# A state-space scan with two attention and feed-forward layers: the last feed-forward chunk on two row tiles, and the attention sums one step later

## The chip, the core and the metric

The kernel runs on one core of a Trainium2 chip. A core has five engines with queues of their own: PE, the matrix engine (its weight loads are listed as PEld); DVE, the vector engine; ACT, the scalar engine; POOL, the general engine (GpSimd); and SP (SyncE), which here only issues transfers. Each takes its instructions in the order in which they were queued, and they meet at semaphores. Operands lie in on-chip memory (SBUF); PE writes into accumulator banks (PSUM). The metric is the device time of one execution, in microseconds (us).

## The reference

The input `x` holds 32 sequences of 256 tokens with 256 features, in fp32. The result is `x` plus what two stages make of it. Cut to what matters:

```python
# stage 1, once: a gated state-space block
xr, gate = split(x @ W_in.T); xr = xr + cond[:, None, :]
xn = layernorm(silu(causal_conv4(xr)))               # 512 channels
Bm, Cm, dt = split(xn @ W_xproj.T)                   # 16 states each
h = clip(h * (1 + dt*A) + Bd * xn_t, -10, 10)        # 256 steps, one after another
y = (C_t . h + D * xn) * silu(gate) @ W_out.T

# stage 2, two layers of:
q, k, v = split(shift_token(y) @ wqkv)               # 8 heads of 64
q, k = rotary_xpos(l2norm(q) * qs, l2norm(k) * ks)
y = y + softmax(local_mask(8 * q @ k.T)) @ v @ wo     # windows of 128, each sees the one before
h = layernorm(shift_token(y)) * lg + lb
a, g = split(h @ w1 + b1)                            # 682 each
y = y + (a * gelu(g)) @ w2 + b2                      # 682 -> 256
```

## The kernel before

**Groups and the order of work.** The 32 sequences are handled in four groups of eight (`GB`). A generator, `group_scan`, emits stage 1 of one group as an agenda of small pieces, in chunks of 32 time steps. Another, `blocks`, emits stage 2 of a group and yields after each slot of work. `side_by_side` runs the two together: while `blocks` does the layers of group g, pieces of the scan of group g+1 are emitted between its slots, about one and a half per slot. So the scan of group 0 runs alone at the start, three groups have a scan beside them, and the last group has none. The order in which a queue gets its instructions follows from this emission; the tile framework, which adds the semaphores, moves some of them a little.

**Attention.** `blocks` goes over the eight sequences `b` of the group (L1184). Work for b and b+1 is mixed in eight slots, so that PE has other work while the remaining engines prepare what it needs next:

- slots 1, 2, 4, 5 project v, q and k of sequence b+1, window by window (`project_qkv`, L736). `rotated` (L745 to L770) then makes the normalised and rotated q or k: a square on ACT (L749), multiplies and sums on DVE (L752, L757, L762, L766), an addition, a power and a multiply on POOL (L760, L768, L769).
- `turn(b, w)` transposes the rotated q and k of one window on PE (L775), and ACT copies them out of PSUM (L780). Window 1 of b is turned in slot 1 of b; window 0 of b+1 in slot 8 of b.
- slot 3 divides sequence b-1 by its sums (`divide`, PE L994, DVE L1002), and computes scores; `scores` (L926 to L952) first puts the mask into the bank with a bf16 matmul (L934), then runs heads in pairs, one on rows 0 to 63 and one on rows 64 to 127 of the array (L941). ACT takes the exponential (L950). The last scores come in slot 6.
- slot 6 also runs `finish(b-1)`, the output projection (L786) and its addition to the residual.
- slot 7 runs `sums(b)`: PE adds the exponentials over the keys (`rs`, L960) and DVE takes the reciprocal (L968); and `values(b)`: the exponentials times v (`ov`, L979), copied by ACT (L986).

For the last two sequences of a group the first two sequences of the feed-forward are prepared in the same slots. `normalise(0, n)` transposes the residual (`tp_h`, L1019), takes mean and variance on DVE, the inverse root on POOL (L1029), and normalises (`hn`, DVE L1031). `spread(0, n)` transposes the result back (`tp_hn`, L1044).

**Feed-forward.** `feed_forward` takes two sequences at a time (index j, 512 tokens). The 682 hidden columns are cut into `MCH`, five chunks of 128 and one of 42 rows (`MREM`). `widen(j, m)` computes both halves of chunk m (L1066), ACT applies gelu (L1074), and DVE multiplies, giving `ag` (L1076). `narrow(j, m)` multiplies `ag` with `w2` into two PSUM banks `po_f0` and `po_f1`, one for each half of the 256 output features (L1087), added up over the six chunks. It runs one chunk behind `widen`, except that the last chunk follows at once: `widen(j, 5)`, then `narrow(j, 4)`, then `narrow(j, 5)`. In the last pair of a layer the first projections of the next layer and a `turn` come in between (`lead_in`). In `widen` the 42-row chunk already keeps both halves side by side, on two column tiles: one at rows 0 to 41 of a bank, the other from row `DH` = 64.

**Weights.** `ff_weights` (L1146) loads `w1` and `w2` of a layer, one buffer each, by SP (L1137). Behind them in SP's queue are the loads `xrep` (L538), which bring the scan its next rows.

An fp32 matmul is executed as two passes, each with its own weight load, so counts of PE instructions in the profile are twice those in the code.

Of the kernel before, what the change touches and what calls it, by code (L numbers as in the profile page):

```python
# [14 lines left out]
ALU = mybir.AluOpType  # L15
# [4 lines left out]
P = 128  # L20
S = 256
DM = 256
KM = DM // P
# [14 lines left out]
DH = 64  # L38
W = 128
NW = S // W  # L40
HID = 682
MCH = [(o, min(P, HID - o)) for o in range(0, HID, P)]
MREM = MCH[-1][1]
# [30 lines left out]
def kernel(  # L74
# [29 lines left out]
    nc = tc.nc  # L104
# [5 lines left out]
    def loaded(src, shape, name, q=None):  # L110
        t = const.tile(shape, FP, tag=name, name=name)
        (q or nc.scalar).dma_start(out=t, in_=src)
        return t
# [18 lines left out]
    b1_sb = loaded(b1, [P, L, 2, len(MCH)], "b1_sb")  # L132
# [20 lines left out]
    for j in range(NJ):  # L153
# [25 lines left out]
        out=mask_t[:, 0:W], in_=mask_t[:, 0:W], compare_op=ALU.is_ge, fill=MASKED_LOW,  # L179
# [3 lines left out]
        out=mask_t[:, W : 2 * W], in_=mask_t[:, W : 2 * W], compare_op=ALU.is_ge,  # L183
# [9 lines left out]
    for h in range(HEADS):  # L193
# [7 lines left out]
        out=b1g_sb[DH : DH + MREM], in_=b1[0:MREM, :, 1, len(MCH) - 1]  # L201
# [12 lines left out]
    with tc.tile_pool(name="setup", bufs=2) as setup, tc.tile_pool(  # L214
# [3 lines left out]
        for src, pos, dst in ((qk_scale, rot_c, rc_sb), (qk_scale_sw, rot_s, rs_sb)):  # L218
            tab = setup.tile([P, NW, 2, DH], FP, tag="tab", name="tab")
            nc.scalar.dma_start(out=tab, in_=pos)  # L220
            for l in range(L):
                sc = setup.tile([P, 2 * DH], FP, tag="qk_sc", name="qk_sc")
                nc.scalar.dma_start(
                    out=sc, in_=src[l].rearrange("a d -> (a d)").partition_broadcast(P)
# [63 lines left out]
    def program(ctx, exact):  # L288
# [12 lines left out]
        def bank(pool, tag, name):  # L301
            return pool.tile([P, DI], FP, tag=tag, name=name)
# [493 lines left out]
        if exact:  # L796
# [4 lines left out]
                out=mask[:, 0:W], in_=mask[:, 0:W], compare_op=ALU.is_ge, fill=MASKED,  # L801
# [3 lines left out]
                out=mask[:, W : 2 * W], in_=mask[:, W : 2 * W], compare_op=ALU.is_ge, fill=MASKED,  # L805
# [201 lines left out]
        class FeedForward:  # L1007
# [46 lines left out]
            def widen(self, j, m):  # L1054
                l, (o, n) = self.l, MCH[m]
                pa = bank(ps_w, "w", "pa")
                if n == P:
                    pg, b1g = bank(ps_w, "w", "pg"), b1_sb[0:n, l, 1, m : m + 1]
                    order = [(x, k) for x in (1, 0) for k in range(KM)]
                else:  # L1060

                    pg, b1g = pa[DH : DH + n], b1g_sb[DH : DH + n, l : l + 1]
                    order = [(x, k) for k in range(KM) for x in (1, 0)]
                for half_, k in order:
                    ps = pg if half_ else pa
                    nc.tensor.matmul(  # L1066
                        ps[0:n, :],
                        self.w1[:, k, half_ * HID + o : half_ * HID + o + n],
                        self.h[j][:, k].rearrange("p b t -> p (b t)"),
                        start=(k == 0),  # L1070
                        stop=(k == KM - 1),
                    )
                gl = aw.tile([P, 2 * S], FP, tag="pT", name="gl", bufs=6)
                nc.scalar.activation(gl[0:n, :], pg[0:n, :], AF.Gelu, bias=b1g)  # L1074
                ag = aw.tile([P, 2 * S], FP, tag="pT", name="ag", bufs=6)
                nc.vector.scalar_tensor_tensor(  # L1076
                    ag[0:n, :], pa[0:n, :], b1_sb[0:n, l, 0, m : m + 1], gl[0:n, :],
                    ALU.add, ALU.mult,
                )
                self.ag[m] = ag  # L1080

            def narrow(self, j, m):
                if m == 0:
                    self.po = [bank(ps_w, "w", f"po_f{d}") for d in range(KM)]
                n = MCH[m][1]
                for d in range(KM):
                    nc.tensor.matmul(  # L1087
                        self.po[d],
                        self.w2[0:n, m, d * P : (d + 1) * P],
                        self.ag[m][0:n, :],  # L1090
                        start=(m == 0),
                        stop=(m == len(MCH) - 1),
                    )
                if m < len(MCH) - 1:
                    return
                l, b0 = self.l, self.g * GB + 2 * j
                for d in range(KM):
                    po = self.po[d].rearrange("p (b t) -> p b t", b=2)
                    rv = self.res[j][:, d, :, 1:]
                    if l < L - 1:  # L1100
                        nc.vector.scalar_tensor_tensor(
                            rv, po, b2_sb[:, l, d : d + 1], rv, ALU.add, ALU.add
                        )
                    else:
                        xs = ap_.tile([P, 2, S], FP, tag="rot", name="xs", bufs=4)
                        nc.sync.dma_start(out=xs, in_=xT[:, d, b0 : b0 + 2, :])
                        fo = ap_.tile([P, 2, S], FP, tag="swp", name="fo", bufs=3)
                        nc.vector.scalar_tensor_tensor(
                            fo, po, b2_sb[:, l, d : d + 1], rv, ALU.add, ALU.add
                        )  # L1110
                        nc.gpsimd.tensor_add(fo, fo, xs)
                        nc.sync.dma_start(out=outT[:, d, b0 : b0 + 2, :], in_=fo)
# [22 lines left out]
        def weights(src, l, shape, name):  # L1135
            t = wpool.tile(shape, FP, tag=name, name=name)
            nc.sync.dma_start(out=t, in_=src[:, l])  # L1137
            return t

        def attention_weights(l):  # L1140
            return (
                weights(wqkv, l, [P, KM, 3 * DI], "wqkv_sb"),
                weights(wo, l, [P, NC_, DM], "wo_sb"),
            )

        def ff_weights(l):  # L1146
            return (
                weights(w1, l, [P, KM, 2 * HID], "w1_sb"),
                weights(w2, l, [P, len(MCH), DM], "w2_sb"),
            )  # L1150

        def scratch(g):
            return dp.tile([P, KM, GB, S], FP, tag="ys", name="ys", bufs=2)
# [26 lines left out]
        def blocks(g, at, nxt):  # L1180

            for l in range(L):
                ff = FeedForward(g, l, at.res, *ff_weights(l))
                for b in range(GB):  # L1184
                    more = b + 1 < GB
                    more and at.project(b + 1, 0, 2)
                    at.turn(b, 1)
                    yield
                    more and at.project(b + 1, 0, 0)
                    more and at.project(b + 1, 0, 1)  # L1190
                    yield
                    b > 0 and at.divide(b - 1)
                    at.scores(b, 1, 0, HEADS // 2)
                    yield
                    at.scores(b, 0, 0, 2)
                    more and at.project(b + 1, 1, 2)
                    yield
                    more and at.project(b + 1, 1, 0)
                    more and at.project(b + 1, 1, 1)
                    yield  # L1200
                    at.scores(b, 0, 2, 2)
                    b > 0 and at.finish(b - 1)
                    if b >= GB - 2:
                        ff.normalise(0, 2 * (b - GB + 2))
                    yield
                    at.sums(b)
                    at.values(b)
                    if b >= GB - 2:
                        ff.normalise(0, 2 * (b - GB + 2) + 1)
                        ff.spread(0, 2 * (b - GB + 2))  # L1210
                    yield
                    more and at.turn(b + 1, 0)
                    if b >= GB - 2:
                        ff.spread(0, 2 * (b - GB + 2) + 1)
                    yield
                yield
                at.divide(GB - 1)
                yield
                res, follow = at.res, None

                def last(m):
                    nonlocal follow
                    if m == 0:
                        if l + 1 < L:
                            follow = Attention(l + 1, res, *attention_weights(l + 1))
                        else:
                            follow = nxt()
                    if follow is not None:
                        lead_in(follow, m)

                pieces = feed_forward(ff, last)
                next(pieces)
                at.finish(GB - 1)
                yield
                for _ in pieces:
                    yield
                at = follow
            state_at[0] = at
# [3 lines left out]
        for _ in group_scan(0, ys):  # L1242
            pass
        at = Attention(
            0, [load_res(ys, j) for j in range(GB // 2)], *attention_weights(0)
        )
        for m in range(6):
            lead_in(at, m)
        for g in range(NG):
            if g + 1 < NG:  # L1250
# [3 lines left out]
                def nxt():  # L1254
                    return Attention(
                        0, [load_res(ys, j) for j in range(GB // 2)], *attention_weights(0)
                    )
# [4 lines left out]
            at = state_at[0]  # L1262
# [119 lines left out]
```

## Time and profile before

Three runs took 4258.27, 4266.41 and 4266.48 us; the median is 4266.41. The profiled execution took 4264.77 us, with a span of 4262.5.

| engine | busy us | share of the span |
|---|---|---|
| PE | 3885.2 | 91% |
| DVE | 2600.1 | 61% |
| ACT | 1744.2 | 41% |
| POOL | 1684.0 | 40% |

| stretch, us | what runs | PE busy, us |
|---|---|---|
| 0 to 510 | the scan of group 0 alone | 379.1 |
| 510 to 3565 | groups 0 to 2, each beside the scan of the next | 2829.0 |
| 3565 to 4262 | group 3 alone | 677.1 |

How to read the lines that follow. A line of the list of groups has the source line, the engine, the operation, what it writes and reads, shapes and count; then busy time and the mean length of one in ns; then the idle time of the engine ahead of it and what ended it. A line of the waits has who waited, for whom, total us, how often, and the longest. A line of the timeline has start, length, engine, line, operation and count. Passes on PE overlap in the pipeline: the length of one is more than the distance to the next start, and the distance is what a pass costs. `42*128` is rows times columns of the array that are used.

### The profile page before, as it was taken

The numbers are of one execution on the slowest core, as the hardware profiler recorded it, in microseconds if no ns is written. First come the engines' busy times: TensorE is split into PE (matmuls) and PEld (weight loads), VectorE is DVE, ScalarE is ACT, GpSimd is POOL, SyncE is SP. The second block draws the span as 40 slices with busy tenths as digits, with TensorE's granted clock in tenths as the row PEclk, the third lists the DMA queues.
The fourth block names the chain that finished last, engine by engine and source line by source line (L and its number), as shares of the span: only waits on it lengthen the run. The fifth ranks groups of instructions, "written<-read, shape, count | busy, mean of one in ns | idle before, by whom it ended". The sixth has DMA issues, their size and how long they took to land. (4 is left out here: it accounts for less than half of the span.)

```text
span 4262.5 us, 51606 instructions
## 1 busy us (share of the span) xinstructions
PE 3885.2 (91%) x17980; PEld 2003.9 (47%) x17980; DVE 2600.1 (61%) x4952; ACT 1744.2 (41%) x3217; POOL 1684.0 (40%) x1749
## 2 busy tenths in 40 slices
PE   5777799898898999999899999999989899999999
PEld 2222255544455445544455445554455544654653
DVE  5777557666676546766776645766677653443442
ACT  2554335443444334443444423544344433322331
POOL 3333165323553156422555126532355314523531
PEclk9899999999999999999999999999999999999999
DMA  5777603443334312443433521344333431000000
GB/s 150 178 185 180 155 24 85 119 104 105 92 92 120 100 57 56 111 108 94 115 95 96 140 67 39 85 119 104 105 95 90 127 95 51 1 20 21 1 10 31
DMA packets 266114, 386.30 MB, mean 91 GB/s; under 512 B 161779, under 2 KB 170996, under 8 KB 263668
## 3 DMA queue, kind: packets, MB, share of 16 engines
q1 hardware_dynamic: 261776, 380.86, 34.1%
q8 instruction: 145, 2.38, 0.2%
q10 hardware_dynamic: 4068, 2.04, 0.2%
q14 instruction: 125, 1.02, 0.1%
HBM read 347.70 MB, written 33.55 MB: 89 GB/s over the span
## 5 line engine op out<-in xcount | busy, mean ns | idle before, releaser
L543 ACT ACTIVATE xrep<-xrep,beta 128x512 f32<-128x512 f32 x1024 | 693.1, 715 | 929.2 <-DMA xrep<-xnd 797.2
L550 DVE CUSTOM_DVE_ANT_0 h<-h,xrep,lim 128x512 f32<-128x512 f32 x1024 | 916.4, 895 | 149.7 <-ACT xrep L543 58.5
L736 PE MATMUL ps_qkv<-wqkv_sb,res 128*128 128x512 f32 x1536 | 733.6, 616 | 16.9 <-DMA res<-ys 6.3
L760 POOL TENSOR_TENSOR rot<-rot,swp 128x512 f32<-128x512 f32 x256 | 331.1, 1293 | 586.8 <-DVE swp L757 503.5
L736 PEld LDWEIGHTS ps_qkv<-wqkv_sb,res 128*128 128x128 f32 x1536 | 287.5, 196 | 359.4 <-issue 303.3
L562 PE MATMUL y<-h,ly 128*32 128x512 f32 x2048 | 411.3, 632 | 48.9 <-DVE h L550 48.0
L768 POOL TENSOR_TENSOR rn<-ss,neg_half 128x8 f32<-128x8 f32 x256 | 434.2, 1696 | 26.5 <-DVE ss L766 14.1
L1087 PE MATMUL po_f<-ag,w_sb 128*128 128x512 f32 (+1 forms) x768 | 378.8, 617 | 37.8 <-DVE ag L1076 37.8
L752 DVE TENSOR_TENSOR rot<-ps_qkv,rc_sb 128x512 f32<-128x512 f32 x256 | 175.6, 686 | 369.2 <-ACT sq L749 369.0
L326 PE MATMUL ps_in<-xg,w_in_sb 128*128 128x256 f32 x1024 | 393.0, 517 | 1.8 <-DMA xg<-in_xT_dram 1.5
L1066 PE MATMUL pa<-hT,w_sb 128*128 128x512 f32 (+1 forms) x896 | 363.8, 596 | 0.0
L1076 DVE SCALAR_TENSOR_TENSOR ag<-pa,b_sb,gl 128x512 f32<-128x512 f32 x192 | 143.4, 747 | 329.9 <-PE pa L1066 210.3
L1066 PE MATMUL pg<-hT,w_sb 128*128 128x512 f32 x640 | 313.7, 613 | 0.0
L769 POOL TENSOR_TENSOR rot<-rot,rn 128x512 f32<-128x512 f32 x256 | 276.7, 1081 | 19.1
L326 PEld LDWEIGHTS ps_in<-xg,w_in_sb 128*128 128x128 f32 x1024 | 190.1, 199 | 187.4 <-issue 127.1
L1029 POOL TENSOR_TENSOR rstd<-ve,neg_half 128x1 f32<-128x1 f32 x128 | 76.5, 598 | 508.1 <-DVE ve L1027 494.5
L373 DVE SCALAR_TENSOR_TENSOR acc<-xr,wc_sb,acc 128x256 f32<-128x256 f32 x384 | 190.0, 506 | 126.7 <-POOL acc L362 122.7
L1087 PEld LDWEIGHTS po_f<-ag,w_sb 128*128 128x128 f32 (+1 forms) x768 | 141.6, 194 | 229.4 <-issue 143.6
L950 ACT ACTIVATE pT<-sc 128x512 f32<-128x512 f32 x384 | 206.2, 590 | 97.1 <-PE sc L941 96.4
L786 PE MATMUL ps_wo<-oT,wo_sb 128*128 128x256 f32 x1024 | 237.3, 385 | 0.0
L583 POOL TENSOR_TENSOR xd<-xd,dskip_sb 128x512 f32<-128x512 f32 x64 | 86.8, 1357 | 367.1 <-DMA xd<-xnd 202.4
L749 ACT ACTIVATE sq<-ps_qkv 128x512 f32<-128x512 f32 x256 | 148.9, 594 | 200.7 <-PE ps_qkv L736 147.5
(144 smaller groups left out, 5444.2 us busy)
## 6 DMA issues: line engine op xcount, KB each, us to landing
xrep<-xnd SPq DMA_DIRECT2D x512, 512.0 KB
xnd<-xn SPq DMA_DIRECT2D x64, 256.0 KB
xd<-xnd SPq DMA_DIRECT2D x256, 64.0 KB
wqkv_sb<-in_wqkv_dram SPq DMA_DIRECT2D x8, 1536.0 KB
w_sb<-in_w_dram SPq DMA_DIRECT2D x8, 1364.0 KB
xg<-in_xT_dram SPq DMA_DIRECT2D x64, 128.0 KB
ys<-yo SPq DMA_DIRECT2D x64, 128.0 KB
res<-ys SPq DMA_DIRECT2D x32, 256.0 KB
```

Source lines behind the costliest of these rows:

```text
L326: nc.tensor.matmul(ps, w_in_sb[:, k, ch * P : (ch + 1) * P], x, start=(k == 0), stop=(k == KM - 1),)
L543: nc.scalar.activation(bx, bx, AF.Copy, scale=ck[c]["beta"][:, t : t + 1])
L550: nc.vector._custom_dve(TENSOR_ADD_SAT, out=h_new, in0=state["h"], in1=bx, s0=ck[c]["lim"][:, 0, t : t + 1], s1=ck[c]["lim"][:, 1, t : t + 1],
L562: nc.tensor.matmul(ck[c]["y", hb][32 * q : 32 * q + 32, :], ly[hb % 2][:, 32 * t : 32 * t + 32], ck[c].pop(("h", hb * TB + t)), start=(i = ...
L736: nc.tensor.matmul(ps, res[b // 2][:, k, b % 2, t0 : t0 + W], wqkv_sb[:, k, a * DI : (a + 1) * DI], start=(k == 0), stop=(k == KM - 1),)
L760: nc.gpsimd.tensor_add(rot, rot, swp)
L768: nc.gpsimd.tensor_tensor(rn, ss, neg_half, ALU.pow)
L769: nc.gpsimd.tensor_mul(rot, rot, bc(rn, 2, DH))
L786: nc.tensor.matmul(po[:, d], wo_sb[:, c, d * P : (d + 1) * P], oT[:, c, :], start=(c == 0), stop=(c == NC_ - 1),)
L950: nc.scalar.activation(p, banks[r], AF.Exp)
L1066: nc.tensor.matmul(ps[0:n, :], self.w1[:, k, half_ * HID + o : half_ * HID + o + n], self.h[j][:, k].rearrange("p b t -> p (b t)"), start= ...
L1087: nc.tensor.matmul(self.po[d], self.w2[0:n, m, d * P : (d + 1) * P], self.ag[m][0:n, :], start=(m == 0), stop=(m == len(MCH) - 1),)
```

## The change

It has two parts, and a transfer that the first needs.

The first part puts the second matmul of the 42-row chunk on two row tiles of the array. Until now both outputs read rows 0 to 41. Now output 0 uses weights and products at rows 0 to 41 and output 1 those at rows 64 to 105, as the scores do with two heads, so that the two may run at the same time. For that DVE makes the product twice, into both places of `ag`, and a small transfer puts a second copy of the last chunk of `w2` at rows 64 to 105.

The second part exchanges slots 7 and 8 of the attention: the transposes of the next sequence's q and k come ahead of the sums and values of this one. They give ACT more time to finish the exponentials that the sums read. The preparations for the feed-forward stay in the slots in which they were.

```diff
 def widen(self, j, m):
...
                     ALU.add, ALU.mult,
                 )
+                if n < P:
+
+                    nc.vector.scalar_tensor_tensor(
+                        ag[DH : DH + n, :], pa[0:n, :], b1_sb[0:n, l, 0, m : m + 1],
+                        gl[0:n, :], ALU.add, ALU.mult,
+                    )
                 self.ag[m] = ag
...
 def narrow(self, j, m):
...
                 for d in range(KM):
+
+                    r0 = 0 if n == P else d * DH
                     nc.tensor.matmul(
                         self.po[d],
-                        self.w2[0:n, m, d * P : (d + 1) * P],
-                        self.ag[m][0:n, :],
+                        self.w2[r0 : r0 + n, m, d * P : (d + 1) * P],
+                        self.ag[m][r0 : r0 + n, :],
                         start=(m == 0),
                         stop=(m == len(MCH) - 1),
                     )
...
         def ff_weights(l):
-            return (
-                weights(w1, l, [P, KM, 2 * HID], "w1_sb"),
-                weights(w2, l, [P, len(MCH), DM], "w2_sb"),
-            )
+            w1_sb = weights(w1, l, [P, KM, 2 * HID], "w1_sb")
+            w2_sb = weights(w2, l, [P, len(MCH), DM], "w2_sb")
+            last = len(MCH) - 1
+            nc.sync.dma_start(out=w2_sb[DH : DH + MREM, last], in_=w2[0:MREM, l, last])
+            return w1_sb, w2_sb
...
                     yield
-                    at.sums(b)
-                    at.values(b)
+                    more and at.turn(b + 1, 0)
                     if b >= GB - 2:
                         ff.normalise(0, 2 * (b - GB + 2) + 1)
                         ff.spread(0, 2 * (b - GB + 2))
                     yield
-                    more and at.turn(b + 1, 0)
+                    at.sums(b)
+                    at.values(b)
                     if b >= GB - 2:
                         ff.spread(0, 2 * (b - GB + 2) + 1)
                     yield
```

## The prediction

> **What bounds the kernel now.** I read four views in this order. First the page's busy times, for the engine that sets the end; then busy time by stretch, because the kernel has two regimes; then what the matrix engine (PE) waits for; last its timeline where the diff touches it.
>
> ```profile
> PE 3885.2 (91%) x17980; PEld 2003.9 (47%) x17980; DVE 2600.1 (61%) x4952; ACT 1744.2 (41%) x3217; POOL 1684.0 (40%) x1749
> ```
> ```profile
> 510.00:3565.00 3055.00, 2828.96 (x13471) 1490.15 (x13472) 1953.57 (x3691) 1300.05 (x2419) 1267.62 (x1300) 0.96 0.36 94
> 3565.00:4262.50 697.50, 677.11 (x3330) 371.30 (x3328) 288.70 (x560) 219.61 (x396) 268.89 (x226) 0.99 0.05 16
> ```
> The columns are stretch, length, and busy PE, PEld, DVE, ACT, POOL. From 510 to 3565 us three groups are transformed while the next group's scan runs in the gaps: PE idles 226 us of 3055 and DVE is 64% busy. The last group has no scan; PE idles 20 of 697 us. So PE is the bound, and a gain is either less PE work or less PE waiting.
>
> ```profile
> PE rs L960 <- ACT pT L950: 49.1, 20, 8.5
> PE tp_hn L1044 <- DVE hn L1031: 42.6, 24, 4.6
> PE po_f L1087 <- DVE ag L1076: 37.8, 13, 5.6
> PE tr_qk L775 <- POOL rot L769: 22.7, 9, 3.6
> ```
> These are PE's waits between 510 and 3565 us. Line 1 is what the second half of the change goes for; line 3 is the piece that its first half touches; lines 2 and 4 are waits that the new order can lengthen.
>
> **What the skill says.** The Trainium skill, TensorEngine Tiling (Array Packing), Key Properties: row tiles work independently, loads and matmuls in parallel, and a change of tiling mode drains the engine. The trace agrees: eight 64-row score matmuls with 256 columns, on two row tiles, take 1.14 us where eight full-height passes at half of the 0.43 us of a 512-column pass would take 1.72; and the first matmul after a mode change comes 0.52 us after the one before, not 0.43. The same page, Gotcha 1, says that different row tiles may not use one PSUM bank at once: the two outputs po_f0 and po_f1 are separate banks, as the two score banks are. TensorE: Matmul & The Clock Gate, Part 1, says that the clock halves after an idle window: passes after a 4.15 us wait start 0.85 apart, not 0.43. The same page says that VectorE takes its queue strictly in order: so the second product stands ahead of the next scan step.
>
> **Part A, the 42-row chunk on two row tiles.** An fp32 matmul is two passes here; the 32 pieces give 128.
>
> ```profile
> L1087 PE MATMUL po_f<-ag,w_sb 42*128 42x512 f32 x128 | 74.2, 706 | 37.8 <-DVE ag L1076 37.8
> L1076 DVE SCALAR_TENSOR_TENSOR ag<-pa,b_sb,gl 42x512 f32<-42x512 f32 x32 | 23.7, 740 | 76.8 <-ACT gl L1074 76.8
> ```
> ```profile
> 865.38 3.78 PE L1087 MATMUL po_f<-ag,w_sb 42*128 42x512 f32 x4 [4.15 <-DVE ag L1076]
> 869.09 3.78 PE L1066 MATMUL pg<-hT,w_sb 128*128 128x512 f32 x4
> ```
> ```profile
> 3916.40 1.98 PE L1087 MATMUL po_f<-ag,w_sb 42*128 42x512 f32 x4
> 3918.31 1.98 PE L736 MATMUL ps_qkv<-wqkv_sb,res 128*128 128x512 f32 x4
> ```
> ```profile
> 4004.99 1.14 PE L941 MATMUL sc<-qT,kT 64*128 64x256 f32 x8
> ```
> One piece holds PE 1.91 us (3918.31 less 3916.40), half clocked 3.71. A pair that ran wholly side by side would save two passes, 0.86 us. But the second output now reads the copy of the product at rows 64 and up, which DVE makes after the first: another 0.74 us (row above; starts follow 0.68 apart). So its start is the later of the first pass and the end of the second product. Going through the 32 pieces by when the first product ended:
> - 4 pieces, after a layer's last turn: it ended 2.9 us ahead. Full 0.86 each, 3.4.
> - 10 pieces ended 0.34 ahead, with no wait: second tile starts about 0.4 late, saving 0.5 each, 4.9.
> - 4 ended 0.2 ahead: 0.33 each, 1.3.
> - 8 where PE waits for the product at full clock: second tile 0.7 late, so 0.72 + 0.45 + 0.52 = 1.7 against 1.91: 0.2 each, 1.8.
> - 6 with a half clock: 0.75 + 1.02 + 0.96 = 2.7 against 3.71: 1.0 each, 6.0.
>
> Sum 17.4 us. Bounds: nothing if the tiles don't pair (the second output started 0.96 after the first before, later than its product will be ready), and 32 x 0.86 plus another 0.86 for the six, 33, if DVE were never late. The added products are 32 x 0.74 = 23.7 us of DVE. Eight lie in the last group, where DVE is 41% busy; the others mostly stand ahead of a scan step, but the feed-forward stretches are PE's (211.6 of 225 us and 169.6 of 170 busy in the first group), so I charge 2 us. Kept: 15.
>
> **The added weight copy.** Eight small transfers on SyncE, each behind a wait for the w2 load, with the scan's row loads (L538) queued behind. w2 lands 4.5 to 6.3 us after issue (transfer updates in the trace). In the second layers one row load stands between, and the next was held for its buffer to 1050.7, w2 having landed at 1045.2; in the first layers the next in the queue are raw-sum turns issued after 1552, w2 having landed at 1551.0. Cost 0; the bound, if all six beside a scan stalled it by 6 us, is 36.
>
> **Part B, sums behind the rotary transposes.** The work is the same; PE now turns b+1 (1.04 us) before it needs the exponentials.
>
> ```profile
> 1235.88 0.62 PE L960 MATMUL rs<-pT,head_cols 128*32 128x256 f32 x4
> 1237.64 1.55 PE L960 MATMUL rs<-pT,head_cols 128*32 128x256 f32 x28 [1.13 <-ACT pT L950]
> 1239.12 2.82 PE L979 MATMUL ov<-pT,v_sb 128*64 128x256 f32 x32
> 1241.87 1.07 PE L562 MATMUL y<-h,ly 128*32 128x512 f32 x8
> 1242.86 3.80 PE L326 MATMUL ps_in<-xg,w_in_sb 128*128 128x256 f32 x8
> 1246.49 1.05 PE L775 MATMUL tr_qk<-ident,rot 128*128 128x128 f32 x8
> ```
> Undisturbed, sums take 1.5 us; here 3.3. Turn and scan work (last three lines) can move into that hole. The excess over 1.5, summed over all 64, is 79 us, more than the listed 49 because it holds slow-clock passes. The turn itself won't wait: the rotated q and k of b+1, first window, left POOL at least 0.7 us before the new place in every block, usually 4 to 14. By sequence:
> - b=0 of first layers and of the last group's second: 5 x 0.8 = 4.0. b=2, 3 beside the scan: 1.2 + 3.2.
> - b=4, 5 of second layers: the whole excess, 8.8.
> - b=0 of second layers: 30 us, but ACT itself is late there behind row loads; only about 1.3 of work moves in: 4.
> - b=6: the transpose of the normalised rows, `spread(0,0)`, used to have sums and values (4.3) ahead of it; now only the turn.
>
> ```profile
> 4101.07 0.41 PE L1044 MATMUL tp_hn<-ident,hn 128*128 128x128 f32 x2
> 4104.64 0.41 PE L1044 MATMUL tp_hn<-ident,hn 128*128 128x128 f32 x2 [2.28 <-DVE hn L1031]
> ```
> Its rows were ready at 4100.93; the new place is 4097.9, so 3.1 of waiting replaces the 2.28 of the second, which hides under values: -0.8. Beside the scan rows were ready at 772.8 and 1330.2, long after: -1 and -1.7, three of each. b=7 likewise moves a wait from its second spread to its first: 0, +/- 2. Together about -10.
>
> Sum 21.2 - 10 = 11; the scan, coupled to PE through in-order queues, can take part back as waits elsewhere: I keep 8. Bounds: -10 with no gain kept, +21 with no loss.
>
> **Forecast**: 4266.4 - 15 - 0 - 8 = 4243; rounded to 4244 (-0.5%).
>
> **Rivals.**
> - Second half worth nothing: its waits only change names, to `tp_hn` and the scan's `y`. For: 30 of the 79 us is late ACT. Against: the 4 us at b=0 lie where nothing else is late. 4266 - 13 = 4253.
> - The second product becomes the wait: 13 listed waits for ag say DVE is already last; 4266 - 5 + 0 = 4261.
> - Slower: spreads wait in all b=6 and 7 (-10), the gain of sums is lost, the weight copy holds up row loads by 2 to 3 us six times (-15), A saves 10: 4281. For: SyncE's queue is in order. Against: the landings above.
> - All of it kept: A with the clock staying up 20, B 21: 4225.
>
> **Chances.** Forecast 0.47, second half nothing 0.20, DVE wait 0.14, slower 0.10, all kept 0.09. The 0.2% lines are 4257.9 and 4274.9. Faster: 0.46 + 0.16 + 0.02 + 0.09 = 0.73; within: 0.01 + 0.04 + 0.12 + 0.02 = 0.19; slower 0.08. The range 4226 to 4270 leaves out most of the slower case and the best of the last.
>
> **What would show it.** Right: 42-row passes in pairs a few ns apart or 0.4 apart; PE's time at them down by some 17 us; sums at 1.5 us in b=0, 4, 5; `tp_hn` waits longer at the first spread of b=6, 7 and gone at the second. Wrong: four 42-row passes still in a row at 0.43; `po_f` waits for the line of the second product growing by more than 8 us; row loads late after each w2; PE idle between 510 and 3565 us not below 226.

## The result, and the profile after

| kernel | median us | runs | lowest to highest |
|---|---|---|---|
| before | 4263.86 | 4 | 4258.27 to 4266.48 |
| after | 4235.37 | 4 | 4226.95 to 4242.98 |

The ratio is 0.9934, 95% interval 0.9912 to 0.9957: 28 us faster, against a forecast of 22 (the kernel before has one run more here than in the section on its time). A second series, with the experiments, gave 0.9932 (0.992 to 0.9944), so the size is firm. The profiled execution after has a span of 4234.9 us.

First the page's busy times, then the busy time by stretch. The bounds of the stretches are moved to the same work: the third mixed group now ends at 3540, not at 3565.

```profile
PE 3858.7 (91%) x17980; PEld 1998.1 (47%) x17980; DVE 2624.4 (62%) x4984; ACT 1744.8 (41%) x3217; POOL 1692.1 (40%) x1749
```
```profile
510.00:3540.00 3030.00, 2807.05 (x13480) 1483.76 (x13480) 1974.25 (x3718) 1301.53 (x2421) 1277.70 (x1303) 0.97 0.36 95
3540.00:4234.90 694.90, 671.45 (x3320) 370.76 (x3320) 291.11 (x564) 218.20 (x394) 265.43 (x224) 0.98 0.05 15
```
PE still bounds the kernel, and DVE has its added 24 us. In the mixed stretch PE idles 3030.0 - 2807.1 = 223 us; before it was 226. So of the 25 us gained there only 3 are idle time, though the wait of the sums was the aim of the second part. The rest is in busy time. These are PE's waits in that stretch after the change:

```profile
PE tp_hn L1044 <- DVE hn L1031: 41.1, 12, 7.9
PE po_f L1095 <- DVE ag L1076: 35.7, 12, 5.0
PE sc L934 <- DVE swp L757: 30.2, 26, 3.5
PE tr_qk L775 <- POOL rot L769: 24.2, 10, 3.9
PE rs L960 <- ACT pT L950: 16.6, 3, 5.7
```
The sums' wait fell from 49.1 us in 20 places to 16.6 in 3. The wait for the normalised rows is as large as before, but in 12 places and up to 7.9 us long instead of 24 places and 4.6. The scores' wait for the rotary multiplies (swp) rose from 19.0 to 30.2.

Where did busy time go? I took the time from each PE start to the next, less the listed wait, and summed it by what is written (my sums over the trace, us):

```
            before   after   difference
po_f         354.7   340.5     -14.2    second matmul
rs           116.0   104.6     -11.4    sums
rb           122.3   112.4      -9.9    broadcast of the reciprocals
pg           287.5   284.3      -3.2
ov           180.6   185.0      +4.4
sc           319.6   324.1      +4.5
ps_raw        68.6    72.4      +3.8
```
The first line is the first part of the change. The next two come from waits that are gone, though they are not waits themselves. A run of sums that was held up in its middle took 2.1 us beside its wait, not 1.44. Most of the difference is the four passes ahead of the wait, which then hold PE to their modelled end: 0.62 us, where four in a run take 0.18. And at the last sequence of a mixed group's layer the eight `rb` passes, soon behind a wait, ran wholly or in part at half the clock: 2.3 to 3.6 us against 1.74 to 1.92 after. `ov`, `sc` and others give a part back. The two do not count alike: `rs` falls by 11.4 us also in the experiment below that keeps the exchange for b = 0 to 5 alone and gains nothing by it, while 7.4 us of the fall of `rb` lie at b = 7 of the mixed groups.

The 42-row chunk, by the groups list and then the timeline of PE (one of DVE):

```profile
L1095 PE MATMUL po_f<-ag,w_sb 42*128 42x512 f32 x128 | 60.1, 731 | 36.0 <-DVE ag L1076 35.7
L1082 DVE SCALAR_TENSOR_TENSOR ag<-pa,b_sb,gl 42x512 f32<-42x512 f32 x32 | 23.8, 744 | 1.0
```
```profile
3886.39 1.13 PE L1095 MATMUL po_f<-ag,w_sb 42*128 42x512 f32 x4
3887.45 1.13 PE L736 MATMUL ps_qkv<-wqkv_sb,res 128*128 128x512 f32 x2
```
```profile
867.11 2.85 PE L1095 MATMUL po_f<-ag,w_sb 42*128 42x512 f32 x4 [3.36 <-DVE ag L1076]
869.89 1.22 PE L1066 MATMUL pg<-hT,w_sb 128*128 128x512 f32 x1
```
```profile
866.31 0.74 DVE L1076 SCALAR_TENSOR_TENSOR ag<-pa,b_sb,gl 42x512 f32<-42x512 f32 x1 [0.90 <-ACT gl L1074]
867.09 0.74 DVE L1082 SCALAR_TENSOR_TENSOR ag<-pa,b_sb,gl 42x512 f32<-42x512 f32 x1
```
Where both products are long ready (3886.39), two pairs hold PE for 1.06 us instead of 1.91. Where PE waits for the first product (867.11), the second begins only 0.78 after it (867.09 less 866.31), and the piece holds PE 2.78 instead of 3.71.

The sums of the piece that the prediction showed (second layer, b = 4), and then the first normalised rows of b = 6 in the last group with the sums behind them:

```profile
1229.86 1.05 PE L775 MATMUL tr_qk<-ident,rot 128*128 128x128 f32 x8
1230.85 1.06 PE L562 MATMUL y<-h,ly 128*32 128x512 f32 x8
1231.84 3.80 PE L326 MATMUL ps_in<-xg,w_in_sb 128*128 128x256 f32 x8
1235.57 1.51 PE L960 MATMUL rs<-pT,head_cols 128*32 128x256 f32 x32
```
```profile
4070.58 0.69 PE L1044 MATMUL tp_hn<-ident,hn 128*128 128x128 f32 x2 [3.27 <-DVE hn L1031]
4071.20 2.79 PE L960 MATMUL rs<-pT,head_cols 128*32 128x256 f32 x32
```
In the first, turn and scan stand ahead of the sums, which run in 1.51 us with no wait, as forecast. In the second the rows are waited for 3.27 us, where 3.1 was forecast, and the sums behind take 2.79 us.

To find where the 28 us lie I aligned the kernels by landmarks (the start of each output projection and of each pair's first widening). The table gives the change of length against before, in us, over the three mixed groups; each is from one profile. Entries of the first layers' attention wander by some 3 us; those of the second layers by more: two kernels below, in the order of before and no slower or faster, show -8.4 and -1.9 at b = 0 to 3 and -1.9 and -5.5 at b = 7. The columns other than "both (after)" are experiments.

| place | row tiles alone | exchange alone | both (after) | exchange for b 0 to 5 | for b = 7 | for some |
|---|---|---|---|---|---|---|
| 1st layer, b = 0 to 3 | 0.1 | -0.5 | 2.0 | -1.1 | 0.2 | -0.3 |
| 1st layer, b = 4, 5 | -2.2 | **14.0** | **12.6** | **13.6** | -1.7 | -2.2 |
| 1st layer, b = 6 | -1.1 | 10.2 | 10.0 | 2.0 | -0.1 | 0.0 |
| 1st layer, b = 7 | -0.4 | -16.0 | -16.0 | -0.4 | -6.3 | -4.9 |
| 1st layer, feed-forward | -9.7 | -2.8 | -12.3 | -5.8 | -10.6 | -9.1 |
| 2nd layer, b = 0 to 3 | -6.0 | -8.0 | -7.1 | -7.4 | -5.6 | -9.9 |
| 2nd layer, b = 4, 5 | 1.7 | -10.9 | -10.4 | -10.9 | 4.0 | -11.7 |
| 2nd layer, b = 6 | 1.1 | 5.8 | 6.5 | -4.1 | -3.0 | 1.2 |
| 2nd layer, b = 7 | -0.5 | -14.3 | -14.9 | -1.6 | -5.4 | -13.5 |
| 2nd layer, feed-forward | -0.8 | -1.0 | 1.3 | 0.0 | 0.9 | 3.9 |
| last group, all | -0.6 | 4.6 | 1.6 | -2.0 | 0.5 | 0.4 |

In the first layers the large entries come back in every kernel with the same order: 11.0 to 13.9 at b = 4 and 5, 9.6 to 10.3 at b = 6, and -16.0 at b = 7 wherever 6 and 7 are both exchanged. A second profile of the changed kernel has -8.5, 3.1 and -13.9 in the second layers, against -10.4, 6.5 and -14.9.

### The profile page after: what moved, and what is told of

Same layout as the page of the kernel before. It is cut to its first block, busy times and chain, and to the rows that moved or that the text cites. A ratio compares the mean times of both kernels' runs of the same rounds, so it can differ in the third digit from the quotient of the medians.

```text
span 4234.9 us, 51632 instructions
## 1 busy us (share of the span) xinstructions
PE 3858.7 (91%) x17980; PEld 1998.1 (47%) x17980; DVE 2624.4 (62%) x4984; ACT 1744.8 (41%) x3217; POOL 1692.1 (40%) x1749
## 3 DMA queue, kind: packets, MB, share of 16 engines
q14 instruction: 125, 1.02, 0.1%
## 5 line engine op out<-in xcount | busy, mean ns | idle before, releaser
L562 PE MATMUL y<-h,ly 128*32 128x512 f32 x2048 | 410.1, 636 | 49.1 <-DVE h L550 48.2
L768 POOL TENSOR_TENSOR rn<-ss,neg_half 128x8 f32<-128x8 f32 x256 | 433.3, 1692 | 27.1 <-DVE ss L766 14.9
L1095 PE MATMUL po_f<-ag,w_sb 128*128 128x512 f32 (+1 forms) x768 | 364.7, 622 | 36.0 <-DVE ag L1076 35.7
L941 PE MATMUL sc<-qT,kT 64*128 64x128 f32 (+1 forms) x2048 | 227.4, 352 | 0.4
```

The lines of the kernel that those rows point to most:

```text
L562: nc.tensor.matmul(ck[c]["y", hb][32 * q : 32 * q + 32, :], ly[hb % 2][:, 32 * t : 32 * t + 32], ck[c].pop(("h", hb * TB + t)), start=(i = ...
L768: nc.gpsimd.tensor_tensor(rn, ss, neg_half, ALU.pow)
L941: nc.tensor.matmul(banks[r][:, i, :], kT[rows, i0 + i, kw * W : (kw + 1) * W], qT[rows, i0 + i, kw * W :], start=False, stop=(i == n - 1),)
L1095: nc.tensor.matmul(self.po[d], self.w2[r0 : r0 + n, m, d * P : (d + 1) * P], self.ag[m][r0 : r0 + n, :], start=(m == 0), stop=(m == len(MC ...
```

## Experiments

All ratios are to the kernel before on the same chip, with their 95% intervals.

**The changed kernel again, and its parts.** 

> The changed kernel once more, on the chip of the next three, as their mark. My theory and its rivals agree here: the ratio to the kernel before is within 0.15% of the 0.9934 of the result (0.992 to 0.995).

> The row tiles alone, with the added product and weight copy; sums, values and transposes in the order of before. My theory: the pairs save 17 us of PE time and DVE takes 2 back: 15 us, ratio 0.9965. Rival, the second product becomes the wait: 5 us or less, ratio 0.999 or more. Rival, the whole gain of the change is here and the second part only renames waits: 26 to 28 us, ratio 0.9935. In the profile of my theory the waits of the sums for the exponentials stay at 49 us between the start and the end of the mixed stretch.

> The exchange of the two slots alone, the 42-row chunk as before. My theory: 21 us of sums gained, 10 lost at the first normalised rows of the sequences 6, and some handed back to the scan: 8 to 11 us, ratio 0.9975 to 0.998. Rival, its waits only change names: 0 to 2 us, ratio 0.9995 to 1. Rival, it is what brought most of the gain: 20 us or more, ratio 0.9953 or less.

| run | ratio | us |
|---|---|---|
| after again | 0.9932 (0.992 to 0.9944) | -28 |
| row tiles alone | 0.9975 (0.9967 to 0.9983) | -11 |
| exchange alone | 0.9962 (0.995 to 0.9975) | -14 to -16 |

The parts add up: 11 + 14 to 16 = 25 to 27 of 28, within the noise. So neither hides the other, and the forecast had the shares the wrong way round: 15 and 8. The exchange lies past my theory's range, between it and the largest rival.

**The exchange for sequences 0 to 5 only.** 

> The changed kernel with the exchange of slots for sequences 0 to 5 only; for 6 and 7, beside which the first rows of the feed-forward are normalised, sums and values stay ahead of the transposes. My theory: the loss of 10 us at the sequences 6 does not occur, and the small gains of sums at 6 and 7 are lost: 5 to 9 us less than the changed kernel, ratio to before 0.992; waits for the normalised rows at the first of the two transposes fall from 5 to 8 us back to under 2.5. Rival, what waits there would have waited later anyway (the scan sets the pace beside it): no difference to the changed kernel within 2 us.

```diff
-                    more and at.turn(b + 1, 0)
+                    if b < GB - 2:
+                        more and at.turn(b + 1, 0)
+                    else:
+                        at.sums(b)
+                        at.values(b)
...
-                    at.sums(b)
-                    at.values(b)
+                    if b < GB - 2:
+                        at.sums(b)
+                        at.values(b)
+                    else:
+                        more and at.turn(b + 1, 0)
```
0.9968 (0.9957 to 0.9979), which is 16 us worse than the changed kernel and no better than the row tiles alone. Both readings fell, and with them a step of the prediction: at b = 6 and 7 together the exchange does not cost 10 us, it brings all that the second part brings. For 0 to 5 it nets nothing that shows, since the first layers' b = 4 lose 13 and the second layers' gain 11. The timeline of PE at b = 7 of a first layer shows the gain, first in the kernel before:

```profile
798.06 0.62 PE L960 MATMUL rs<-pT,head_cols 128*32 128x256 f32 x4 [0.80 <-ACT yo L640]
799.73 1.55 PE L960 MATMUL rs<-pT,head_cols 128*32 128x256 f32 x28 [1.04 <-ACT pT L950]
801.21 2.82 PE L979 MATMUL ov<-pT,v_sb 128*64 128x256 f32 x32
803.96 0.44 PE L1019 MATMUL tp_h<-ident,res 128*128 128x128 f32 x2
...
809.88 0.66 PE L1044 MATMUL tp_hn<-ident,hn 128*128 128x128 f32 x2 [2.31 <-DVE hn L1031]
810.33 1.96 PE L326 MATMUL ps_in<-xg,w_in_sb 128*128 128x256 f32 x4
812.12 2.46 PE L994 MATMUL rb<-rinv,head_rows 128*128 128x256 f32 x8
```
and the same place after the change:

```profile
804.87 0.38 PE L1019 MATMUL tp_h<-ident,res 128*128 128x128 f32 x2
805.18 1.92 PE L562 MATMUL y<-h,ly 128*32 128x512 f32 x16
808.03 0.41 PE L1044 MATMUL tp_hn<-ident,hn 128*128 128x128 f32 x2 [0.93 <-DVE ve L436]
808.27 1.94 PE L326 MATMUL ps_in<-xg,w_in_sb 128*128 128x256 f32 x4
810.14 1.51 PE L960 MATMUL rs<-pT,head_cols 128*32 128x256 f32 x32
811.58 2.82 PE L979 MATMUL ov<-pT,v_sb 128*64 128x256 f32 x32
814.33 0.44 PE L1044 MATMUL tp_hn<-ident,hn 128*128 128x128 f32 x2
814.61 1.94 PE L326 MATMUL ps_in<-xg,w_in_sb 128*128 128x256 f32 x4
816.37 1.91 PE L994 MATMUL rb<-rinv,head_rows 128*128 128x256 f32 x8
```
There is no turn at b = 7. The second row's transpose for the feed-forward (tp_h, 804.87) now goes ahead of sums and values, and these hide the whole way of its rows over DVE and POOL to the last tp_hn. Both waits of the sums go too. That is 0.80 + 1.04 + 2.31 - 0.93 = 3.2 us of waits, and 0.65 each of `rb` and `rs`; together 4.5 of the 5.3 us by which this place is shorter. In the second layers the sums of b = 7 had no wait; there the wait at the second spread, up to 4.62 us, and the slow `rb` go.

**Where the exchange pays.** 

> Row tiles, and the two slots exchanged for the last sequence of a group (b = 7) alone. The three runs before suggest it: aligned block by block, the exchange takes 16 us out at b = 7 in each layer of the mixed groups, gives 13.7 back at b = 4 of the first layers and 20 at b = 6, and the rest is worth 11 at b = 4, 5 of the second layers. My new theory: 7 alone brings 25 to 30 us beyond the row tiles' 11, ratio 0.9905. Rival, the place where the time is found moves with the order and the total stays: ratio 0.9935 like the changed kernel, or 0.997 like the row tiles alone.

> Row tiles, and the exchange for b = 7 of both layers and b = 0 to 5 of the second layers; not for b = 6 nor for 0 to 5 of the first layers. My new theory: the 11 us of b = 4, 5 come on top of the last kernel, ratio 0.988. Rival, the blocks are not independent: what comes early at 4 and 5 is waited for at 6: no difference to the last kernel, 0.9905.

```diff
-                    more and at.turn(b + 1, 0)
+                    early = b == GB - 1 or (l == 1 and b < GB - 2)
+                    if early:
+                        more and at.turn(b + 1, 0)
+                    else:
+                        at.sums(b)
+                        at.values(b)
```
with the reverse in the next slot, and `early = b == GB - 1` for the first of the two. 7 alone: 0.9945 (0.9931 to 0.9959), 13 us beyond the row tiles, not 25 to 30; that expectation failed, and the rival's first figure, 0.9935, is within the interval. I had counted the 10 and 6 us at b = 6 as a loss apart from the gain at b = 7. In the first layers the two belong together: without an exchange at 6, b = 7 gains 6.3 and, in the selected exchange, 4.9; with it 16.0, and 6 and 7 together give -6.4 in this run against -6.0 in the changed kernel. The first normalised rows of b = 7 are waited for 2.6 us without the exchange at 6 and 0.9 with it. That a wait at 6 lets the engines behind PE catch up is my reading; an exchange at 6 alone was not tried. In the second layers the link does not hold: the selected exchange has none at 6 either, and gains 13.5 at 7 where this run gains 5.4.

The selected exchange: 0.9885 (0.987 to 0.990), the ratio expected, but in part by luck. The expected step was 11 us from 0.9905; the measured one is 26 us, give or take 9, from 0.9945. By place the 12.6 us at the first layers' b = 4 and 5 are gone and the 11.7 of the second layers kept; against the run of 7 alone the second layers are shorter by 16 us at b = 4 and 5 and by 8 at b = 7. So the blocks are not independent, though the other way from the rival; why b = 7 gains more here stays open. The selected exchange beats the changed kernel by 0.5%.

**Why b = 4 of the first layers loses.** 

> The changed kernel, with three copies out of PSUM taken from ACT and given to DVE, once in the first layer of a group: the v of sequence 6, first window, and the transposed q and k of sequence 5, second window. In the changed kernel they stand on ACT behind an xrep multiply that waits about 8 us for its rows, and the same stretch of PE is 12.5 us longer over three groups than before. My theory, the order on ACT is what costs there: those 12.5 us go, 8 to 12 us below the changed kernel, ratio 0.991. Rival, the rows set the pace there whatever stands behind them, or DVE is as late (the multiplies of the rotary wait on its queue): within 3 us of the changed kernel, ratio 0.993 to 0.994.

```diff
-                    nc.scalar.copy(self.qkv[b][2][:, w], ps)
+                    if self.l == 0 and b == 6 and w == 0:
+                        nc.vector.tensor_copy(self.qkv[b][2][:, w], ps)
+                    else:
+                        nc.scalar.copy(self.qkv[b][2][:, w], ps)
```
and the same for the two copies of `turn`. 0.9932 (0.9919 to 0.9946): no change, and the place is still 11 us longer. Those three copies are not what PE waits for. What stays in the trace of this run, ACT, DVE and PE in turn:

```profile
702.70 1.33 ACT L543 ACTIVATE xrep<-xrep,beta 128x512 f32<-128x512 f32 x2 [7.69 <-DMA xrep<-xnd]
...
706.28 0.36 ACT L587 ACTIVATE th_g<-ps_in 128x256 f32<-128x256 f32 x1
```
```profile
706.67 0.42 DVE L593 SCALAR_TENSOR_TENSOR sg<-th_g,ps_in 128x256 f32<-128x256 f32 x1 [6.20 <-ACT th_g L587]
```
```profile
707.15 0.38 PE L941 MATMUL sc<-mask_t,ident_b 128*128 128x512 bf16 x1 [1.31 <-DVE sg L593]
...
711.20 0.39 PE L941 MATMUL sc<-mask_t,ident_b 128*128 128x512 bf16 x1 [0.63 <-DVE swp L757]
713.40 0.39 PE L941 MATMUL sc<-mask_t,ident_b 128*128 128x512 bf16 x1 [1.81 <-DVE swp L757]
```
The gate of the scan (`th_g`) also stands behind the rows on ACT; DVE, in order, idles 6.2 us for it with the rotary multiplies queued behind, and the scores wait for those. That the gate is the cause is read from this chain; it was not tried by itself. That the order causes the loss is shown: every kernel with the exchange there loses 11 to 14 us, every one without it none.

**What the second product costs.** 

> The changed kernel without DVE's second product: output 1 of the 42-row chunk reads rows 64 to 105 of the chunk before, long ready (so the product of the last chunk is left out of output 1). It prices the second product, as a wait and as work on DVE. My theory: full pairs save 0.86 instead of 0.54 a piece on average, some 10 us, and DVE gets 23.7 us back, worth 2: 10 to 12 us below the changed kernel, ratio 0.9905. Rival, the product costs nothing because the pairs are late for another reason: within 3 us, ratio 0.993. Rival, DVE's added 24 us are paid in full by the scan: 25 us or more, ratio 0.9875.

> The kernel before with DVE's second product of the 42-row chunk, which nothing reads. My prediction charged 2 us for it, ratio 1.0005. From the run without the product I now expect 4 to 6 us, ratio 1.001 to 1.0015. Rival, it costs its whole 23.7 us, ratio 1.0055; rival, nothing, 1.000.

```diff
-                        self.ag[m][r0 : r0 + n, :],
+                        self.ag[m - 1 if r0 else m][r0 : r0 + n, :],
```
Without it: 0.9897 (0.9883 to 0.9912), some 15 us below the changed kernel, more than the 10 to 12 expected. Made but not read: 0.9992 (0.9984 to 1.000), the rival "nothing", and not the 4 to 6 us expected. So the 23.7 us of DVE cost nothing that shows, less than the 2 charged, and its lateness costs 15. The time for which the chunk holds PE (first start to the next instruction's start, 31 pieces) agrees: 70.1 us before, 56.4 after, 41.0 without the product. There 29 of the 32 pieces are two full pairs.

**The weight copy.** 

> The kernel before with the second copy of the last chunk of w2, which nothing reads. My theory: nothing, ratio 1.000 (0.999 to 1.001). Rival, it holds up the row loads behind it by 2 to 6 us in each layer: 12 to 36 us, ratio 1.003 to 1.0085.

0.9998 (0.999 to 1.0007). It costs nothing.

**The chunk one step later.** 

> The changed kernel with the last chunk's second matmul one step later: behind the next pair's first widening, for three of a layer's four pairs. Then neither of the two products is waited for. My theory of the first part, that DVE's second product comes too late for a full pair in 28 of the 32 pieces and that the wait for the first costs 36 us beside it: the three moved pieces of a layer save 0.86 each in full and most of the waits go: 20 to 30 us below the changed kernel, ratio 0.987 to 0.989. Rival, what ends the waits for the product is the scan that DVE and PE share, and it ends another wait instead: within 5 us of the changed kernel, ratio 0.9925 to 0.9935.

```diff
                     if m > 0:
                         ff.narrow(j, m - 1)
+                    elif j > 0:
+                        ff.narrow(j - 1, NM - 1)
...
-                    if m == NM - 1:
+                    if m == NM - 1 and j == GB // 2 - 1:
                         ff.narrow(j, m)
```
0.9922 (0.9908 to 0.9935), about 5 us below the changed kernel, though the intervals overlap: the rival. The waits did go, and most came back under another name:

```profile
PE tp_hn L1044 <- DVE hn L1031: 64.8, 24, 7.8
PE sc L934 <- DVE swp L757: 32.2, 29, 3.5
...
PE po_f L1095 <- DVE ag L1076: 7.7, 3, 3.1
```
`po_f` fell from 35.7 to 7.7 us, `tp_hn` rose from 41.1 to 64.8. By place, the feed-forward of the first layers took 38.5 us less than before (changed kernel: 12.3), and the first sequence of the second layers 11.8 more (3.4 less). Three of the moved pieces, 5 us of PE, cross from the one place into the other, so only the sum of the two compares: 27 us less than before, 16 in the changed kernel. Of these 11 us the other places give back about half. In that stretch of the first group (970 to 1105 us) ACT's wait for the scan's rows rose. These are the changed kernel's line and then this kernel's:

```profile
ACT xrep L543 <- DMA xrep<-xnd: 34.0, 14, 4.7
```
```profile
ACT xrep L543 <- DMA xrep<-xnd: 43.0, 16, 7.0
```
**Both improvements together.** 

> The fastest order so far (the exchange for sequence 7, and for 0 to 5 of the second layers) with the last chunk's second matmul one step later as well. If what the later step gains in the feed-forward is given back at the first sequence of the second layer, as it was with the changed kernel: 3 to 6 us below the order alone, ratio 0.987. If the gains add in full (26 us in the mixed groups, 5 in the last): ratio 0.981.

0.9862 (0.9846 to 0.9878), the fastest kernel here. Against the selected order alone, 0.9885, this is some 10 us, between the two expectations. The first, 0.987, lies within the interval; the full sum, 0.981, does not. The first sequence of the second layers is longer again (+10.4 us against -7.5), with the same three pieces in it.

## Why the prediction was right, and where its steps were wrong

*The bound.* Right: PE busy fell by 26.5 us and the end came 28 us earlier.

*Part A.* Mechanism right, size off by 3. The table of pieces gave 17.4; their holds fell by 14.1. Long-ready pieces: 0.86 forecast, 0.85 measured. Those 0.34 ahead: 0.5 against 0.36. Those 0.2 ahead: 0.33 against 0.14. Waiting at full clock: 0.2 against 0.1. Half clock: 1.0 against 0.93. Two terms were mis-sized. The second product begins 0.78 after the first, where I took 0.68 from a run of other starts; and the second output's two passes start 0.53 apart, where I took 0.45. Its DVE cost, put at 2, was nothing measurable. Alone it brought 11 us (7 to 14). The statement of the Trainium skill, TensorEngine Tiling (Array Packing), Key Properties, that row tiles work independently, held: pairs start 0.01 us apart, and without the late product save 0.85 of 1.91.

*The weight copy.* Right, 0.

*Part B.* The total was forecast at 8 and measured at 14 to 16, and by its terms the agreement is poorer than that. Right: b = 4 and 5 of the second layers, 8.8 forecast and 10.4 found. About 4 were forecast for b = 0 there; 3.4 are seen, but 3.5 also with the row tiles alone, so they cannot be put down to the exchange. Nothing came of the 4.0 and 4.4 at b = 0, 2 and 3: the sums of b = 0 and 3 do fall to 1.44 us (b = 2 only from 1.85 to 1.72), but the places as a whole are no shorter.

Not foreseen: the first layers' b = 4, a loss of 12. Wrong: "Together about -10" for b = 6 and 7. The wait at the first spread came (to 7.9 us, more than forecast) and the one at the second went, as "What would show it" said; beside the scan b = 6 became 3.3 and 2.2 us longer, where losses of 1 and 1.7 were forecast. But b = 7 "likewise moves a wait from its second spread to its first: 0, +/- 2" left out two things. First, at b = 7 no turn goes into the hole; what moves ahead of sums and values is the second row's tp_h, so that its long way is hidden and no wait takes the place of the old one (0 to 0.9 us against 2.3 to 4.6 in the mixed groups; in the last group the wait did move, 2.07 to 2.58). Second, I priced the slow passes of the sums, in the excess of 79 us, but not those of `rb` behind the spread, which took up to twice their time: 7.4 us at b = 7 of the mixed groups. In the mixed groups 6 and 7 bring 14 us in place of the loss of 10. That the total came near is luck: a missed gain of some 23 us at 6 and 7 and missed losses of 12 (b = 4), 8 (b = 0, 2, 3) and 4 (last group, in the run of the exchange alone) nearly cancelled.

*The rivals.* "Its waits only change names" gives the right total for b = 0 to 5, though there the second layers gain what the first lose, and is wrong for 7. "The second product becomes the wait" did not come about: its 15 us were taken from a saving of 29 (70.1 less 41.0 above). The sign given for being wrong, idle time "not below 226", came out at 223, and the gain was elsewhere: idle time alone was a poor test.

## What to carry to other kernels

Before an in-order queue is reordered, follow what each slot holds for every pass of its loop: the last sequence, which had no turn, gave most of the gain (13 of 14 to 16 us). Count a wait with the passes that it slows before and after it. And in a stretch where two loops share the engines, test an exchange place by place: here some places paid, others cost nearly as much, and the selection more than doubled what the exchange brought.

## What the runs showed of the hardware

The half clock comes late, and on a grid. The granted clock of PE in these traces (PEclk of the profile) is 1.0 or 0.5. In the kernel before, after the first 515 us, all 44 stretches of half clock start on one grid of 3.41 us, and all but the last, which outlasts the kernel, last 3.41, 6.83 or 10.24 us. In the 42-row pieces of the changed kernel, waits up to 2.39 us left the two passes of an output at their full 0.53 apart (in the kernel without the second product, 2.85 us did). After 3.36 us (the piece at 867.11) the clock halved 0.50 us into the piece: the first output's passes are still 0.55 apart, those of the second, which starts at 0.78 behind its product, 1.01. After 4.09 us and more it had halved by the piece's start, or within 0.1 us of it, and both are 0.99 to 1.02 apart. But a shorter wait can be paid for later. In the kernel before, a wait of 2.33 us ended at 1937.17, its piece ran at full speed, and the clock halved 2.5 us after the wait. One of 2.07 us, among small transposes, ended at 4123.10; the clock halved 1.1 us later, and `rb` took 2.76 us against 1.89. So the length of the one wait does not decide alone. What else does, where it falls on the grid or how little PE did around it, these runs don't separate.

Two row tiles paired even across four passes whose weights differ: with both products ready the starts were 0, 0.01, 0.53 and 0.54, and the next instruction followed at 1.06. That is 0.2 more than two passes of 0.43, as the 1.91 of the four passes in a row was 0.2 more than four.
